# Column masks moved from VectorE to GpSimd, and a tile's shares from two VectorE operations to one on ScalarE

## The chip, the cores and the metric

One core of one Trainium2 chip runs the kernel. Engines are named as in the profile: PE (TensorE; PEld are its weight loads), DVE (VectorE), ACT (ScalarE), POOL (GpSimd) and SP (SyncE, which issues plain DMAs). Times are device microseconds of one execution; less is better. Before the change, nine runs have a median of 751.92 us (750.51 to 753.59).

## The reference

Two things are computed from the same normalized rows and added to the input: a selective scan over rows sorted by cluster, and a mixture of eight experts of which each token takes its two best.

```python
xn = _layernorm(x)                       # x: (2, 2048, 256)
# scan, d_state 16, per batch, in the order of the clusters
buckets = argmax(l2norm(xn) . l2norm(means)); sort_idx = argsort(buckets, stable)
u = xn[sort_idx].T
x_dbl = x_proj_weight @ u
dts, Bm, Cm = split(x_dbl, [32, 16, 16]);  Cm += (means @ prompt_weight.T)[buckets].T
delta = softplus(dt_projs_weight @ dts + bias);  A = -exp(A_logs)
h = exp(delta * A) * h + (delta * u) * Bm        # for each step, 256 channels x 16 states
y = sum over states of h * Cm,  + Ds * u,  back in the order of the tokens
# experts, 8, hidden 512
logits = xn @ w_gate;  top2, sel = top_k(logits, 2);  probs = softmax(top2)
e_out = (silu(xn @ w1) * (xn @ w3)) @ w2         # for the chosen experts
out = x + y + sum of probs * e_out
```

All values are float32.

## The kernel before

**The front (about the first 100 us).** Rows are normalized and written to a DRAM tensor `xn_d` of 256 + 4 columns. Each token's cluster and its two experts are found. `route` gives the pairs of token and expert places in 71 tiles of 128 rows (`NT`), each tile of one expert; inside it `find_weights` (L579) finds each tile's expert, and with it `te8` (the expert's index minus 8), and `find_shares` (L600) finds the two softmax weights of each token. `find_shares` puts four numbers in the last four columns of a row: first expert (minus 8), second weight, first weight minus second weight, second expert. 68 tiles (`n_dealt`) are always run; the last three stand in a conditional branch.

**A tile of the experts (`Tile`, L909).** Its weights come by two indirect DMAs of POOL (`load_up`, `load_down`, L914), its rows by another (`load_rows`, L928). `turn` (L933) transposes the rows on PE, ACT copies them (`xT`, L939), and two DVE operations find `own`, the weight of each row: `(first expert == this tile's) * (first - second) + second` (L941, L945). `up` does 16 matmuls for each half (L954), with a tanh on ACT (L962) and two DVE operations (`silu` L967, `gate` L971); `down` does 8 (L977), ACT scales the result with `own` into `yo` (L981), and POOL adds it to the output by an indirect DMA (L895). There are three weight buffers: `load_up` of tile t+3 follows `up` of tile t. There are four row buffers, three of `yo`, six of `own`.

**The scan (`Piece`, L638, and `Step`, L824).** A piece is 512 positions of one batch; there are eight. A piece has eight steps: four groups `q` of four states, for each half `h` of the channels. A step's four states each need `da` on ACT (L834), a product `bu` (L840) and a scan (L849) on DVE. The results of a step lie interleaved in `hs`; PE turns them (L861), ACT copies them (`ht`, L865), and PE contracts them with C (L870). For that contraction C stands in `z`, a tile of 128 x 512 for each `q`: partition p holds the C of state p mod 4 for all positions (`load_z`, L686, a broadcast DMA of SP), and `mask_z` (L695, the multiplication is L697) makes it zero outside the columns of that partition's own position within a group of 32. There is one buffer for each `q`, so the load for the next piece waits for the last contraction with the old one.

**The order.** `keep_order` (L126) makes every engine, POOL and SP among them, follow the order of the text. The main loop goes over 256 places (64 steps of four). At each place it emits a product, a scan, a part of the step before, then what `plan` has for that place, then as many parts of tiles (`jobs`: the first half of `up`, the second half, `down`) as a planner allows: `at_place` sums an estimate of PE and DVE time for each place (`on_pe`, `on_dve`; a mask counts 0.6 of DVE), and a part is dealt while PE's sum is under `ratio` times DVE's. Masks of the next piece stand at places 22, 27, 33 and 41 of a piece (L1135), those of the first at places 5, 6, 14 and 22 of the whole loop (L1146 to L1149). The `gather` of the next piece's rows (L632) is four more indirect DMAs of POOL, and `add_sums` another four.

Of the kernel before, what the change touches and what calls it, by code (L numbers as in the profile page):

```python
# [48 lines left out]
P = 128  # L49
# [7 lines left out]
def scan_moe_kernel(  # L57
# [27 lines left out]
    TS = P  # L85
    NT = (2 * B * L - E) // TS + E
    SH = 4
    HC = CH // 2
    BJ = B * J
    assert K == E == 8 and R == 32 and L % CH == 0 and H == CH  # L90
# [450 lines left out]
    def route():  # L541


        oh = oh_e
        (m1, m2), (i1, i2) = best, which
        (m1, m2), (i1, i2) = best, which
        cum = sml.tile([P, E, BJ], F32, tag="cum2", name="cum2")
        nc.vector.tensor_tensor_scan(
            cum.rearrange("p e j -> p (e j)"), keep2.rearrange("p e j -> p (e j)"),
            both.rearrange("p e j -> p (e j)"), 0.0, ALU.mult, ALU.add,  # L550
        )
        tot = sml.tile([P, E], F32, tag="tot2", name="tot2")
        nc.vector.tensor_copy(tot, cum[:, :, BJ - 1])
        pn = ps_m.tile([P, 2 * E], F32, tag="m", name="pn2")
        nc.tensor.matmul(pn[:, 0:E], lhsT=before, rhs=tot, start=True, stop=True)
        nc.tensor.matmul(pn[:, E:], lhsT=ones, rhs=tot, start=True, stop=True)
        normalize(n_x - 1, False)
        n_i = sml.tile([P, E], I32, tag="n_i", name="n_i")
        nc.vector.tensor_scalar(n_i, pn[:, E:], float(TS - 1), None, ALU.add)
        nc.vector.tensor_scalar(  # L560
            n_i, n_i, TS.bit_length() - 1, None, ALU.logical_shift_right
        )
        nt = sml.tile([P, E], F32, tag="nt", name="nt")
        nc.vector.tensor_copy(nt, n_i)
        end = sml.tile([P, E], F32, tag="end", name="end")
        nc.vector.tensor_tensor_scan(end, ones[:, 0:E], nt, 0.0, ALU.mult, ALU.add)
        base = sml.tile([P, E], F32, tag="base2", name="base2")
        nc.vector.tensor_sub(base, end, nt)
        nc.vector.tensor_scalar(base, base, float(TS), -1.0, ALU.mult, ALU.add)
        nc.vector.tensor_add(base, base, pn[:, 0:E])  # L570
        nc.vector.tensor_tensor(cum, cum, over(base, BJ), ALU.add)
        at = sml.tile([P, 2, BJ, E], F32, tag="at", name="at_slot")
        for i in range(2):
            nc.vector.tensor_mul(at[:, i], oh[:, i], cum.rearrange("p e j -> p j e"))
        sf = sml.tile([P, 2, BJ], F32, tag="sf", name="sf")
        nc.vector.tensor_reduce(sf, at, AX.X, ALU.add)
        slot = sml.tile([P, 2 * BJ], I32, tag="slot", name="slot")
        nc.vector.tensor_copy(slot, sf.rearrange("p i j -> p (i j)"))
        def find_weights():  # L579

            ge = sml.tile([P, NT, E], F32, tag="ge", name="ge")
            nc.vector.tensor_tensor(
                ge, over(idx_t, E), end.unsqueeze(1).to_broadcast([P, NT, E]), ALU.is_ge
            )
            te = sml.tile([P, NT], F32, tag="te", name="te")
            nc.vector.tensor_reduce(te, ge, AX.X, ALU.add)
            nc.vector.tensor_scalar_min(te, te, float(E - 1))
            nc.vector.tensor_scalar(te8, te, -float(E), None, ALU.add)
            nc.vector.tensor_copy(n_used, end[:, E - 1 : E])

            held = sml.tile([P, NT], F32, tag="held", name="held")
            nc.vector.memset(held[:, 0:NW], 0.0)
            nc.vector.tensor_tensor(held[:, NW:], te[:, NW:], te[:, : NT - NW], ALU.is_equal)
            nc.vector.tensor_scalar(held, held, float(E * P), row_p, ALU.mult, ALU.add)
            nc.vector.scalar_tensor_tensor(w_row, te, float(P), held, ALU.mult, ALU.add)  # L595
            for t in tiles[: NW - 1]:
                t.load_up()
                t.load_down()

        def find_shares():  # L600

            share = sml.tile([P, BJ, SH], F32, tag="share", name="share")
            nc.vector.tensor_copy(share[:, :, 0], i1)
            nc.vector.tensor_copy(share[:, :, 3], i2)
            nc.vector.tensor_sub(m2, m2, m1)
            nc.vector.tensor_mul(m2, m2, rstd)
            nc.scalar.activation(m2, m2, AF.Exp)
            nc.vector.tensor_scalar_add(m1, m2, 1.0)
            nc.vector.reciprocal(m1, m1)
            nc.vector.tensor_mul(share[:, :, 1], m2, m1)  # L610
            nc.vector.tensor_sub(share[:, :, 2], m1, share[:, :, 1])
            for b in range(B):
                nc.sync.dma_start(
                    xn_d[b * L : (b + 1) * L, D:].rearrange("(p j) c -> p j c", j=J),
                    share[:, b * J : (b + 1) * J, :],
                )

        tokens = list_tokens(
            slot, [m * LC // J % B for m in range(2 * BJ // LC)], NT, "e", front_factors,
            [lambda: None, find_shares, lambda: None, find_weights] + [lambda: None] * 3  # L620
            + [lambda: counts.extend(count_members())],
        )
        none = sml.tile([P, NT], F32, tag="none", name="none")
        nc.vector.tensor_scalar(none, tokens, 0.0, spare, ALU.is_equal, ALU.mult)
        nc.vector.scalar_tensor_tensor(token_of, tokens, -1.0, none, ALU.add, ALU.add)
# [12 lines left out]
    class Piece:  # L638
# [55 lines left out]

        def mask_z(self, q: int):  # L695
            z = self.zs[q]
            nc.vector.tensor_mul(z, z, mask.unsqueeze(1).to_broadcast([P, CH // G, G]))  # L697

        def load_b(self, q: int, parts: int = 1):
            bt = scn.tile([P, Q, CH], F32, tag="b", name="bt")  # L700
# [208 lines left out]
    class Tile:  # L909
# [23 lines left out]
        def turn(self):  # L933
            xg = self.xg
            pt = ps_m.tile([P, ND, P], F32, tag="m", name="pt_g")
            for h in range(ND):
                nc.tensor.transpose(pt[:, h, :], xg[:, h * P : (h + 1) * P], ident)
            self.xT = ffn.tile([P, ND, TS], F32, tag="xT", name="xT")
            nc.scalar.copy(self.xT, pt)  # L939
            self.own = ffn.tile([P, 1], F32, tag="own", name="own", bufs=6)  # L940
            nc.vector.scalar_tensor_tensor(  # L941
                self.own, xg[:, D : D + 1], te8[:, self.t : self.t + 1], xg[:, D + 2 : D + 3],
                ALU.is_equal, ALU.mult,
            )
            nc.vector.tensor_add(self.own, self.own, xg[:, D + 1 : D + 2])  # L945

        def up(self, i: int):
            wk = w13_sb[self.t % NW][:, i * ND * H : (i + 1) * ND * H].rearrange(
# [168 lines left out]
    for n, p in enumerate(pieces):  # L1117
        s0 = n * SP_
        for q in range(1, NQ):
            at_place(max(s0 + 2 * q - 3, 0), NSUB - 1 if n or q > 1 else 0, lambda p=p, q=q: p.load_b(q))  # L1120
        if n:
            s1 = s0 - SP_
            at_place(max(s1 - 1, 0), 1 if n > 1 else 0, p.gather)

            at_place(s1 + 3, 2, lambda p=p: behind_down.append(p.size), 1.1)
            for h in range(ND):
                at_place(s1 + 1, 2 + h, lambda p=p, h=h: p.turn(h), 0.5)
                at_place(s1 + 2, 1 + 2 * h, lambda p=p, h=h: p.project(h), 0.55)
                at_place(s1, 18 + 2 * h, lambda p=p, h=h: p.decay_of_one(h))
            at_place(s1, 23, p.log)  # L1130
            for i, place in enumerate((23, 24, 26, 28)):
                at_place(s1, place, lambda p=p, i=i: p.series(i), 0.0, 1.1)
            at_place(s1 + 2, 0, p.find_members, 0.0, 0.5)
            at_place(s1 + 3, 0, p.end_projection, 0.55)
            for q, load, use in ((0, 16, 22), (1, 20, 27), (2, 29, 33), (3, 37, 41)):  # L1135
                at_place(s1, load, lambda p=p, q=q: p.load_z(q))
                at_place(s1, use, lambda p=p, q=q: p.mask_z(q), 0.0, 0.6)
            at_place(s1 + 5, NSUB - 1, lambda p=p: p.load_b(0))
            at_place(s0, 3, lambda p=p: p.begin(0), 0.9)
            at_place(s0 + 1, 1, lambda p=p: p.begin(1), 0.9)  # L1140
        s2 = s0 + SP_
        at_place(s2, 0, lambda p=p: p.take_sums(0))
        if n + 1 < len(pieces):
            at_place(s2, 3, lambda p=p: p.take_sums(1))
            at_place(s2 + 1, 0, p.add_sums)
    at_place(1, 1, lambda: pieces[0].mask_z(0), 0.0, 0.6)  # L1146
    at_place(2, 3, lambda: list_rows(1, pos), 2.5, 4.0)
    for q in range(1, NQ):
        at_place(2 * q - 1, 2, lambda q=q: pieces[0].mask_z(q), 0.0, 0.6)  # L1149

    for n in range(NSUB * len(steps)):
        on_dve[n] += 1.75
# [129 lines left out]
```

## Time and profile before

| | us |
|---|---|
| median of nine runs | 751.92 |
| the profiled execution | 752.49 |
| its span, first to last instruction | 750.7 |
| mean granted TensorE clock | 0.953 |

| group (whole span) | count | busy us | mean ns |
|---|---|---|---|
| DVE scans L849 | 256 | 323.9 | 1281 and 1219 |
| DVE products L840 | 256 | 173.1 | 677 |
| PE matmuls of `up` L954 | 2176 | 272.6 | 281 |
| ACT `da` L834 | 256 | 183.6 | 734 |
| ACT `ht` L865 | 256 | 138.3 | 595 |
| POOL adds to the output L895 | 100 | 197.5 | 1927 and 2077 |
| POOL weight loads L914 | 136 | 185.9 | 1353 and 1382 |
| POOL row loads of tiles L928 | 68 | 91.4 | 1344 |

How to read the profile: "busy" is the time in which an engine has an instruction under way; matmuls and DVE operations overlap their neighbours a little, so what an operation costs is the time from its start to the next one's. A POOL indirect DMA is busy while POOL prepares it; the bytes arrive later. In a timeline a line is: start, length, engine, source line, operation, output and inputs with their shapes, count, and in brackets how long the engine was idle before and what ended that ("issue" is nothing that the profile shows).

### The profile page before, as it was taken

How to read it: one execution, taken by the hardware profiler on the slowest of the kernel's cores; microseconds unless marked ns; L12 is line 12 of the kernel's file. 1: busy time of each engine (PE TensorE's matmuls, PEld its weight loads, DVE VectorE, ACT ScalarE, POOL GpSimd, SP SyncE). 2: the span in 40 equal slices, each digit the busy share in tenths (PEclk: the TensorE clock that was granted, in tenths of full speed). 3: DMA queues.
4: the chain of work that ended last, by engine and by line, in shares of the span. 5: the costliest groups of instructions: out<-in, count | busy, mean ns of one | idle time of the engine just before them, and what ended most of it. 6: DMA issues, size and time to landing. Idle time of an engine off the chain costs nothing. (4 is left out here: it accounts for less than half of the span.)

```text
span 750.7 us, 16877 instructions
## 1 busy us (share of the span) xinstructions
PE 677.5 (90%) x6506; PEld 588.9 (78%) x6506; DVE 678.9 (90%) x1085; ACT 508.6 (68%) x983; POOL 522.2 (70%) x362
## 2 busy tenths in 40 slices
PE   7465779999998999999999999999999998999993
PEld 5234678788877898788878898998798977899982
DVE  8876399899987999999999999999999996999992
ACT  4831446686758866886769577967795767767762
POOL 2023548667777788777877887788788888677734
PEclk9755979999999999999999999999999999999998
DMA  8576554584435745685468546864585547735312
GB/s 269 227 162 244 162 171 92 159 257 133 126 55 163 254 144 121 171 270 140 113 141 271 164 128 122 269 189 127 122 251 155 136 84 224 233 109 120 87 17 29
DMA packets 60401, 120.31 MB, mean 160 GB/s; under 512 B 24160, under 2 KB 41248, under 8 KB 53152
## 3 DMA queue, kind: packets, MB, share of 16 engines
q0 software_dynamic: 38784, 63.71, 35.5%
q1 hardware_dynamic: 21536, 55.50, 21.9%
q8 instruction: 52, 0.85, 0.5%
q14 instruction: 29, 0.24, 0.1%
HBM read 170.78 MB, written 22.28 MB: 257 GB/s over the span
## 5 line engine op out<-in xcount | busy, mean ns | idle before, releaser
L954 PE MATMUL p_ps<-xT,w 128*128 128x128 f32 x2176 | 272.6, 281 | 12.3 <-DVE g L971 8.1
L954 PEld LDWEIGHTS p_ps<-xT,w 128*128 128x128 f32 x2176 | 258.0, 195 | 26.3 <-DVE g L971 8.3
L849 DVE TENSOR_TENSOR_SCAN hs<-da,carry,bu 128x512 f32<-128x512 f32 x192 | 245.9, 1281 | 0.0
L834 ACT ACTIVATE da<-dl,na 128x512 f32<-128x512 f32 x256 | 183.6, 734 | 0.2 <-DVE dl L789 0.2
L840 DVE TENSOR_TENSOR bu<-du,bt 128x512 f32<-128x512 f32 x256 | 173.1, 677 | 0.0
L865 ACT COPY ht<-pt_s 128x512 f32<-128x512 f32 x256 | 138.3, 595 | 39.1 <-PE pt_s L861 38.1
L895 POOL DMA_INDIRECT out_dram<-yo,token_of x68 | 131.0, 1927 | 46.8 <-ACT yo L981 20.2
L914 POOL DMA_INDIRECT w<-in_w_up_dram,w_row x68 | 92.0, 1353 | 93.7 <-DVE w_row L595 44.6
L861 PE MATMUL pt_s<-ident,hs 128*128 128x128 f32 x1024 | 135.9, 276 | 9.4 <-ACT ht L865 8.6
L977 PE MATMUL py<-w,g 128*128 128x256 f32 x544 | 129.8, 381 | 8.0 <-ACT xT L939 4.8
L861 PEld LDWEIGHTS pt_s<-ident,hs 128*128 128x128 f32 x1024 | 116.0, 141 | 20.9 <-ACT ht L865 13.4
L977 PEld LDWEIGHTS py<-w,g 128*128 128x128 f32 x544 | 98.0, 190 | 21.1 <-ACT xT L939 6.0
L928 POOL DMA_INDIRECT xg_sb<-xn,token_of x68 | 91.4, 1344 | 26.2 <-issue 12.2
L914 POOL DMA_INDIRECT w<-in_w_down_dram,w_row x68 | 93.9, 1382 | 20.7 <-issue 15.2
L895 POOL DMA_INDIRECT out_dram<-yt,line_of x32 | 66.5, 2077 | 20.8 <-issue 10.9
L849 DVE TENSOR_TENSOR_SCAN hs<-da,bu 128x512 f32<-128x512 f32 x64 | 78.0, 1219 | 0.0
L962 ACT ACTIVATE t_sb<-p_ps 128x512 f32<-128x512 f32 x68 | 41.0, 603 | 53.7 <-PE p_ps L954 53.5
L870 PE MATMUL y<-ht,z 128*32 128x128 f32 x2048 | 73.8, 277 | 1.8 <-PEq L1208 0.7
L981 ACT ACTIVATE yo<-py,own 128x256 f32<-128x256 f32 x68 | 32.3, 475 | 62.1 <-PE py L977 60.8
L967 DVE SCALAR_TENSOR_TENSOR t_sb<-t_sb,p_ps 128x512 f32<-128x512 f32 x68 | 45.8, 674 | 26.4 <-ACT t_sb L962 26.4
L870 PEld LDWEIGHTS y<-ht,z 128*32 128x32 f32 x2048 | 50.8, 109 | 19.8 <-issue 10.4
L632 POOL DMA_INDIRECT xs<-xn,line_of x32 | 41.8, 1306 | 14.7 <-issue 8.8
(202 smaller groups left out, 583.3 us busy)
## 6 DMA issues: line engine op xcount, KB each, us to landing
bt<-bc SPq DMA_DIRECT2D x31, 1024.0 KB, 5.1
z<-bc SPq DMA_DIRECT2D x32, 256.0 KB, 4.8
xn<-xt SPq DMA_DIRECT2D x8, 520.0 KB, 2.6
xt<-in_x_dram SPq DMA_DIRECT2D x8, 512.0 KB, 7.5
out_dram<-in_x_dram SPq DMA_DIRECT2D x8, 512.0 KB, 8.3
w<-in_w_up_dram,w_row POOLq DMA_INDIRECT x68, 3.9
w<-in_w_down_dram,w_row POOLq DMA_INDIRECT x68, 7.7
xg_sb<-xn,token_of POOLq DMA_INDIRECT x68, 4.5
```

The source lines that it names most:

```text
L834: nc.scalar.activation(self.da[i], self.piece.dl[:, self.h, :], AF.Exp, scale=na[:, self.h, n : n + 1])
L840: nc.vector.tensor_mul(self.bu[i], self.piece.du[:, self.h, :], self.piece.bts[self.q][:, i, :])
L849: nc.vector.tensor_tensor_scan(self.hs[:, :, i], self.da[i], self.bu[i], start, ALU.mult, ALU.add)
L861: nc.tensor.transpose(pt[:, j, :], self.hs[:, t0 : t0 + G, :].rearrange("p t n -> p (t n)"), ident)
L865: nc.scalar.copy(self.ht[i], pt)
L870: nc.tensor.matmul(p.ys[self.h][j * G : (j + 1) * G, i, :], lhsT=p.zs[q][:, i * (P // G) + j, :], rhs=self.ht[i][:, j, :], start=False, st ...
L895: ins = nc.gpsimd.indirect_dma_start(out=out_rows, out_offset=bass.IndirectOffsetOnAxis(ap=numbers, axis=0), in_=rows, in_offset=None, com ...
L914: nc.gpsimd.indirect_dma_start(out=to[self.t % NW], out_offset=None, in_=rows, in_offset=bass.IndirectOffsetOnAxis(ap=w_row[:, self.t : se ...
L928: nc.gpsimd.indirect_dma_start(out=self.xg, out_offset=None, in_=xn_d, in_offset=bass.IndirectOffsetOnAxis(ap=token_of[:, self.t : self.t ...
L954: nc.tensor.matmul(p[:, f, :], lhsT=wk[:, h, f * P : (f + 1) * P], rhs=self.xT[:, h, :], start=h == 0, stop=h == ND - 1,)
L967: nc.vector.scalar_tensor_tensor(self.s, self.s, 1.0, self.p1, ALU.add, ALU.mult)
L977: nc.tensor.matmul(py, lhsT=self.g[:, f, :], rhs=w2[:, f, :], start=f == 0, stop=f == NH - 1)
```

## The change

Three things change. `mask_z` is issued on GpSimd instead of VectorE, at the same places of the written order, and the planner is no longer told of 0.6 of DVE time for it. `own` becomes one ScalarE operation, `Identity(scale * first expert's column + bias)` with the tile's `te8` as scale: a straight line in the expert's index that passes through the first weight at the first expert and the second weight at the second. For that, `find_shares` writes the slope and the offset of that line into the first two of the four columns, which takes eleven VectorE operations instead of eight, and `te8` is the index minus 3.5 (`MID` is 4.5).

```diff
+    MID = (E + 1) / 2
...
-            nc.vector.tensor_scalar(te8, te, -float(E), None, ALU.add)
+            nc.vector.tensor_scalar(te8, te, MID - E, None, ALU.add)
...
             share = sml.tile([P, BJ, SH], F32, tag="share", name="share")
-            nc.vector.tensor_copy(share[:, :, 0], i1)
-            nc.vector.tensor_copy(share[:, :, 3], i2)
             nc.vector.tensor_sub(m2, m2, m1)
             nc.vector.tensor_mul(m2, m2, rstd)
             nc.scalar.activation(m2, m2, AF.Exp)
+            nc.vector.tensor_sub(share[:, :, 3], i1, i2)
+            nc.vector.reciprocal(share[:, :, 3], share[:, :, 3])
             nc.vector.tensor_scalar_add(m1, m2, 1.0)
             nc.vector.reciprocal(m1, m1)
-            nc.vector.tensor_mul(share[:, :, 1], m2, m1)
-            nc.vector.tensor_sub(share[:, :, 2], m1, share[:, :, 1])
+            nc.vector.tensor_mul(share[:, :, 2], m2, m1)
+            nc.vector.tensor_sub(m1, m1, share[:, :, 2])
+            nc.vector.tensor_mul(share[:, :, 0], m1, share[:, :, 3])
+            nc.vector.scalar_tensor_tensor(m1, i2, MID, share[:, :, 0], ALU.add, ALU.mult)
+            nc.vector.tensor_sub(share[:, :, 1], share[:, :, 2], m1)
...
         def mask_z(self, q: int):
             z = self.zs[q]
-            nc.vector.tensor_mul(z, z, mask.unsqueeze(1).to_broadcast([P, CH // G, G]))
+            nc.gpsimd.tensor_tensor(z, z, mask.unsqueeze(1).to_broadcast([P, CH // G, G]), ALU.mult)
...
-            nc.vector.scalar_tensor_tensor(
-                self.own, xg[:, D : D + 1], te8[:, self.t : self.t + 1], xg[:, D + 2 : D + 3],
-                ALU.is_equal, ALU.mult,
-            )
-            nc.vector.tensor_add(self.own, self.own, xg[:, D + 1 : D + 2])
+            nc.scalar.activation(
+                self.own, xg[:, D : D + 1], AF.Identity, bias=xg[:, D + 1 : D + 2],
+                scale=te8[:, self.t : self.t + 1],
+            )
...
-                at_place(s1, use, lambda p=p, q=q: p.mask_z(q), 0.0, 0.6)
+                at_place(s1, use, lambda p=p, q=q: p.mask_z(q))
...
-    at_place(1, 1, lambda: pieces[0].mask_z(0), 0.0, 0.6)
+    at_place(1, 1, lambda: pieces[0].mask_z(0))
...
-        at_place(2 * q - 1, 2, lambda q=q: pieces[0].mask_z(q), 0.0, 0.6)
+        at_place(2 * q - 1, 2, lambda q=q: pieces[0].mask_z(q))
```

## The prediction

> **What bounds the kernel now.** I read the page's shares first.
>
> ```profile
> PE 677.5 (90%) x6506; PEld 588.9 (78%) x6506; DVE 678.9 (90%) x1085; ACT 508.6 (68%) x983; POOL 522.2 (70%) x362
> ```
>
> These are averages over a front without the scan and a long loop, so the loop comes next, in three stretches (busy us of PE, PEld, DVE, ACT, POOL, each with its count).
>
> ```profile
> 100.00:350.00 250.00, 237.85 (x2314) 211.46 (x2313) 233.27 (x337) 175.49 (x346) 188.92 (x124) 0.99 0.56 157
> 350.00:625.00 275.00, 268.52 (x2737) 236.72 (x2736) 268.93 (x374) 204.79 (x399) 224.80 (x142) 1.00 0.62 165
> 625.00:725.00 100.00, 96.51 (x969) 87.56 (x968) 94.51 (x131) 70.85 (x133) 71.42 (x46) 0.98 0.52 132
> ```
>
> From 350 to 625 us PE and DVE are both 98% busy, and ACT 74%. POOL looks free at 82%, but its timeline shows 0.30 us before nearly every DMA: 224.8 + 142 x 0.30 = 267.4 of 275 us. POOL has 7.6 us left in that stretch; three engines are full there, not two. In the first stretch it has 250 - 188.9 - 124 x 0.30 = 24 us.
>
> Why POOL's DMAs are so long is seen by laying its timeline beside DVE's. First POOL:
>
> ```profile
> 113.07 1.91 POOL L914 DMA_INDIRECT w<-in_w_down_dram,w_row  x1 [0.30 <-issue]
> 115.29 0.98 POOL L914 DMA_INDIRECT w<-in_w_up_dram,w_row  x1 [0.31 <-issue]
> ...
> 122.11 1.17 POOL L914 DMA_INDIRECT w<-in_w_up_dram,w_row  x1 [0.31 <-issue]
> 123.58 3.66 POOL L928 DMA_INDIRECT xg_sb<-xn,token_of  x1 [0.30 <-issue]
> ```
>
> and DVE at those moments:
>
> ```profile
> 112.91 1.22 DVE L849 TENSOR_TENSOR_SCAN hs<-da,bu 128x512 f32<-128x512 f32 x1
> ...
> 114.96 0.68 DVE L967 SCALAR_TENSOR_TENSOR t_sb<-t_sb,p_ps 128x512 f32<-128x512 f32 x1
> ...
> 123.53 1.21 DVE L849 TENSOR_TENSOR_SCAN hs<-da,bu 128x512 f32<-128x512 f32 x1
> 124.67 0.65 DVE L840 TENSOR_TENSOR bu<-du,bt 128x512 f32<-128x512 f32 x1
> 125.25 1.21 DVE L849 TENSOR_TENSOR_SCAN hs<-da,bu 128x512 f32<-128x512 f32 x1
> ```
>
> The weight load at 113.07 begins in a scan that ends at 114.13 and lasts until 0.85 us after it; the one at 115.29 begins beside L967, whose second input is in PSUM, and takes 0.98 us. The row load at 123.58 loses three rounds. Over the loop, 246 POOL DMAs that begin under a DVE operation with both inputs in SBUF are 0.51 us longer than the shortest of their kind; 40 that begin beside L967 or L971 are never over 0.05 us longer. So **DVE's two-SBUF-input work and POOL's SBUF reads exclude each other**. Over all 316 DMAs that is 0.40 us each.
>
> **The change, part by part.** The sum starts from the profiled execution, 752.49 us (span 750.7 and 1.8 around it; 0.6 over the median of the runs).
>
> *Masks off DVE.* 32 multiplications of 128x512, mean 664 ns, but each starts 0.58 us before the next DVE operation (294.45 to 295.03): 32 x 0.58 = 18.6 us off DVE.
>
> *Shares off DVE.* L941 and L945 take 0.31 us together from start to start (295.03 to 295.34). 65 of 68 pairs lie in the loop: 20.2 us off DVE.
>
> ```profile
> L697 DVE TENSOR_TENSOR z<-z,mask 128x512 f32<-128x512 f32 x32 | 21.2, 664 | 0.0
> L941 DVE SCALAR_TENSOR_TENSOR own<-xg_sb,te 128x1 f32<-128x1 f32 x68 | 13.8, 203 | 0.0
> L945 DVE TENSOR_TENSOR own<-own,xg_sb 128x1 f32<-128x1 f32 x68 | 10.8, 159 | 2.3
> masks.py:199 POOL TENSOR_SCALAR_AFFINE_SELECT ident<-ident 128x128 f32<-128x128 f32 x1 | 0.3, 293 | 0.1
> ```
>
> *Masks on POOL: their own length.* No such multiplication is in the trace. Low end: DVE's 0.66 us. The nearest POOL row that reads and writes f32 is the select above, 0.293 us for 128 columns, so four times that, 1.17 us, for 512. High end: 1.17 us and the lost rounds above (3.66 - 0.95 = 2.71 us), 3.9 us. I take 1.15 us, next to the select.
>
> *What they take from DVE.* A mask reads two SBUF tensors for all of its length, so I let it hold DVE off that long, in the share of cases where DVE's next operation has two SBUF inputs (246 of 316, some 0.8): 32 x 1.15 x 0.8 = 29 us back on DVE; bounds 0 (no exclusion in this direction) and 37 us. DVE's net is -18.6 - 20.2 + 29 = -10 us. PE, 96% busy over these 625 us, limits what this is worth; I credit 4 us (bounds 0 and, without exclusion, PE's idle of 22).
>
> The Trainium skill's page "GPSIMD Engine Reference", "Performance versus the Vector engine", gives about 2.6 cycles an element to a two-input operation on GpSimd and advises against it; by it a mask would be about 1.17 us, an estimate. Its page "SBUF — State Buffer", "Who interferes with whom", says that a DVE instruction with two SBUF inputs and a GpSimd instruction that reads SBUF block each other for the whole instruction; the trace shows one direction of this, and by the page DVE would lose some 37 us to the masks, which leaves next to nothing of the relief.
>
> *What they take from POOL.* Each adds 0.30 (gap) + 0.40 (mean wait for DVE) + 1.15 = 1.85 us. They stand in the written order, mostly behind a tile's weight load; behind each wait the row gathers, the adds and the next weight loads. 14 masks fall in 350 to 625: 25.9 us, less 2.5 us of DMA waits that DVE's masks caused (0.52 us at 11 starts in all, 14 of 32 masks). Against 7.6 us free, POOL falls 16 us behind there, and some 4 us before. What is late next is the up weights: in 440 to 600 us they are issued 12.7 to 14 us ahead of their first use by PE, and land in 3.9 us (median), so about 9 us can be absorbed. 20 - 9 = 11 us would reach PE; a stalled PE lets DVE idle and shortens POOL's waits, so I take 7.5 us. Bounds: at 0.66 us a mask (c = 1.36) POOL falls 9 us behind in the stretch and nothing reaches PE; the high end is worked out as a rival.
>
> *The first mask.* POOL's order puts it behind the up load that ends at 123.28. PE first uses that z at 121.32 (the first contraction, PE's timeline):
>
> ```profile
> 121.32 1.08 PE L870 MATMUL y<-ht,z 128*32 128x128 f32 x32
> ```
>
> 123.3 + 0.4 + 1.15 = 124.8: PE waits 3.5 us, behind it the next tile and the next turns. DVE idles 2.3 + 1.0 us at 133 to 135 anyway, so I count 2.5 us (0 to 6, if it loses rounds as the DMA at 123.58 did). The second is reached at 131 and used at 144; from the second piece on masks come 40 us or more before their use. Their z is loaded over 10 us earlier (issued at 283.17, masked at 294.45 on DVE, reached by POOL after 305): no wait on SP's queue.
>
> *Shares on ACT.* One ACTIVATE of one column with pointer scale and bias: L429 has that form at 256 columns, 587 ns, one every 0.495 us; L855, four columns without pointers, 195 ns. I take 0.28 us: 65 x 0.28 = 18 us on ACT, 72% busy in the loop. But all 20 us of waits that PE's queue shows in the loop end on ACT, and copies of ht stand behind the new instruction. Bounds 0 and 6 us (a third of the 18); I take 2. What hides the rest is ACT's idle time, its waits for PE.
>
> *Front.* The shares get five new DVE operations (0.22, 0.39 for a reciprocal, 3 x 0.25) and lose two copies (0.17); 0.30 of it fits in the wait for Exp: +0.9, taken as 0.8, since DVE is dense behind it (0 to 1). The pairs there (71.68 to 72.32) precede 4 us of waiting: nothing.
>
> *The planner.* Without 0.6 for each mask its DVE total goes from 597.0 to 577.8; following its sums, 122 of 197 tile parts move, mostly by one place, at most four. All still fit: 0, within 2 either way.
>
> Sum: 752.5 - 4 + 7.5 + 2.5 + 2 + 0.8 = **761 us**, slower by 1.2%. Its own range, with POOL's term from 0 to 20: 753 to 774.
>
> **Rivals.**
>
> 1. *POOL's lateness never reaches PE; relief wins.* For: today PE waits for no weights. Against: 7.6 us free. With 7 of DVE's 10 us credited, and 1 each for the first mask and ACT: 752.5 - 7 + 1 + 1 + 0.8 = 748 us. It decides if c stays under 1.4 us.
> 2. *DVE is not held by a mask.* Then DVE loses 39 us of work, PE's 22 us of idle can shrink by 15, and the first mask and ACT cost 3: 752.5 - 15 + 3 + 0.8 = 741 us. Against: the exclusion of the timelines.
> 3. *A mask is starved as the DMA at 123.58 was.* 2.5 us each, c = 3.2: 14 x 3.2 - 10 = 35 us in the middle stretch and, with some 21 us usable before it, 14 x 3.2 - 2.5 - 21 = 21 before; 56 - 9 = 47, of which PE's stalls return a third: 752.5 + 31 = 783 us. Against: only 11 of the 246 starts lost a further round.
> 4. *The share on ACT is not one operation but brings table loads*, 1.283 us each (L743, L834). For: Ln and Exp alternate there. Against: Identity (L739) runs between Exps without one. At most 7 more: 761 + 4 = 765 us.
>
> **How the numbers follow.** Forecast 0.50 (slower 0.47, same 0.03); rival 1 0.18 (faster 0.14, same 0.04); rival 2 0.08, faster; rival 3 0.16, slower; rival 4 0.08 (slower 0.07, same 0.01). About 0.2% can be told from no change here. Faster 0.22, same 0.08, slower 0.70. The range 743 to 784 leaves out most of rival 2 and the upper half of rival 3, some 0.15.
>
> **What would show it.** Masks on POOL of about 1.15 us plus waits; DVE scans or products near 2.3 us at 32 places; POOL without free time from 350 to 625 and PE waiting for w there; PE waiting for z at 121 us; one ACT instruction of 0.2 to 0.4 us for each tile and no more table loads. It is wrong if DVE's operations keep their length beside a mask, or if PE never waits for a weight.

## The result, and the profile after

| | before | after |
|---|---|---|
| median, us | 752.13 (62 runs) | 805.37 (20 runs, 799.87 to 812.25) |
| ratio, 95% | | 1.0702 (1.0682 to 1.0721) |
| profiled execution, us | 752.49 | 812.37 |
| its span, us, and granted clock | 750.7, 0.953 | 810.6, 0.924 |

The change costs 53 us, against a forecast of 8.5 and a range that ended at 784. Ratios, here and below, come from undisturbed runs alone, and so differ a little from the quotients of the medians beside them; the profiled executions of after and of after_again are not among these and lie 7 us above their medians. First the engines' shares of after, then three stretches of its loop (busy us of PE, PEld, DVE, ACT, POOL, each with its count, then clock, DMA share and GB/s).

```profile
PE 696.2 (86%) x6506; PEld 601.5 (74%) x6506; DVE 673.7 (83%) x920; ACT 527.6 (65%) x1051; POOL 586.7 (72%) x394
```

```profile
100.00:350.00 250.00, 223.23 (x2076) 196.21 (x2076) 207.87 (x246) 164.59 (x338) 191.44 (x121) 0.93 0.47 133
350.00:625.00 275.00, 250.52 (x2453) 221.73 (x2451) 239.83 (x270) 196.43 (x388) 227.44 (x139) 0.96 0.57 157
625.00:725.00 100.00, 91.48 (x895) 79.57 (x897) 88.30 (x101) 68.85 (x141) 81.27 (x53) 0.97 0.60 166
```

From 350 to 625 us DVE has fallen from 98% to 87% and PE from 98% to 91%; POOL is as busy as before. DVE was relieved of 165 instructions and is hardly less busy for it: 673.7 us in all, after 678.9. Both now wait. The waits of PE in the loop (us in total, times, longest), in which before had none for a DMA or for `z`:

```profile
PE p_ps L958 <- DMA w<-in_w_up_dram,w_row: 16.9, 4, 10.6
PE pt_u L658 <- DMA xs<-xn,line_of: 12.1, 8, 3.2
...
PE y L875 <- POOL z L702: 8.6, 1, 8.6
...
PE py L981 <- DMA w<-in_w_down_dram,w_row: 3.6, 4, 1.6
```

All four are POOL's deliveries: 41 us. By the start of each step's first scan, after lies 11 us behind before at the 4th step of 64 (behind the first mask), 12 at the 12th, 19 at the 20th, 34 at the 36th and 57 from the 52nd on: the loss builds up over most of the loop.

The groups (busy us, mean ns, then idle before):

```profile
L854 DVE TENSOR_TENSOR_SCAN hs<-da,carry,bu 128x512 f32<-128x512 f32 x192 | 254.0, 1324 | 0.0
L845 DVE TENSOR_TENSOR bu<-du,bt 128x512 f32<-128x512 f32 x256 | 192.7, 753 | 0.0
...
L854 DVE TENSOR_TENSOR_SCAN hs<-da,bu 128x512 f32<-128x512 f32 x64 | 78.1, 1221 | 0.0
...
L702 POOL TENSOR_TENSOR z<-z,mask 128x512 f32<-128x512 f32 x32 | 42.3, 1323 | 0.8
L946 ACT ACTIVATE own<-xg_sb,te 128x1 f32<-128x1 f32 x68 | 27.0, 397 | 0.0
```

A mask takes 1.32 us on POOL, a share 0.40 us on ACT. Scans and products sum to 524.8 us, 27.8 more than before. Where that comes from is seen at one mask; POOL first, then DVE at that time (start, length):

```profile
333.58 1.03 POOL L919 DMA_INDIRECT w<-in_w_down_dram,w_row  x1 [0.30 <-issue]
334.63 1.28 POOL L702 TENSOR_TENSOR z<-z,mask 128x512 f32<-128x512 f32 x1
336.08 1.30 POOL L919 DMA_INDIRECT w<-in_w_up_dram,w_row  x1 [0.16 <-issue]
```

```profile
333.56 0.66 DVE L975 SCALAR_TENSOR_TENSOR g<-t_sb,p_ps 128x512 f32<-128x512 f32 x1
334.14 2.33 DVE L845 TENSOR_TENSOR bu<-du,bt 128x512 f32<-128x512 f32 x1
336.40 1.27 DVE L854 TENSOR_TENSOR_SCAN hs<-da,carry,bu 128x512 f32<-128x512 f32 x1
```

The weight load got in beside L975, whose second input is in PSUM, and the mask followed it after 0.02 us. The product at 334.14 is held until the mask ends at 335.91, and lasts 2.33 us instead of 0.67.

The first mask, on POOL, DVE and PE:

```profile
121.72 3.91 POOL L919 DMA_INDIRECT w<-in_w_down_dram,w_row  x1 [0.30 <-issue]
125.93 1.00 POOL L919 DMA_INDIRECT w<-in_w_up_dram,w_row  x1 [0.31 <-issue]
126.96 1.27 POOL L702 TENSOR_TENSOR z<-z,mask 128x512 f32<-128x512 f32 x1
```

```profile
121.85 1.21 DVE L854 TENSOR_TENSOR_SCAN hs<-da,bu 128x512 f32<-128x512 f32 x1
122.98 0.65 DVE L845 TENSOR_TENSOR bu<-du,bt 128x512 f32<-128x512 f32 x1
123.57 1.21 DVE L854 TENSOR_TENSOR_SCAN hs<-da,bu 128x512 f32<-128x512 f32 x1
```

```profile
128.28 1.94 PE L875 MATMUL y<-ht,z 128*32 128x128 f32 x32 [8.59 <-POOL z L702]
```

The mask itself is not late by its own length: the weight load two places ahead of it met three DVE operations in a row with both inputs in SBUF, and lasts 3.91 us instead of 1.0.

The longest single wait of PE, 10.6 us, has the same root. POOL, then part of DVE, then PE:

```profile
581.33 7.95 POOL L900 DMA_INDIRECT out_dram<-yt,line_of  x1 [0.31 <-ACT ht L870]
589.58 2.05 POOL L900 DMA_INDIRECT out_dram<-yt,line_of  x1 [0.30 <-issue]
591.93 5.61 POOL L900 DMA_INDIRECT out_dram<-yt,line_of  x1 [0.30 <-issue]
597.85 1.55 POOL L900 DMA_INDIRECT out_dram<-yt,line_of  x1 [0.30 <-issue]
599.70 1.07 POOL L919 DMA_INDIRECT w<-in_w_up_dram,w_row  x1 [0.30 <-issue]
```

```profile
581.28 1.27 DVE L854 TENSOR_TENSOR_SCAN hs<-da,carry,bu 128x512 f32<-128x512 f32 x1
...
586.61 1.27 DVE L854 TENSOR_TENSOR_SCAN hs<-da,carry,bu 128x512 f32<-128x512 f32 x1
587.81 0.65 DVE L971 SCALAR_TENSOR_TENSOR t_sb<-t_sb,p_ps 128x512 f32<-128x512 f32 x1
```

```profile
602.37 6.54 PE L958 MATMUL p_ps<-xT,w 128*128 128x128 f32 x32 [10.62 <-DMA w<-in_w_up_dram,w_row]
```

The add that begins at 581.33 waits through seven scans and products without a gap and gets in beside L971, the first operation with an input in PSUM. It takes 7.95 us where the shortest add takes 1.55. The up weights stand behind it. In before, the loop had 6 POOL DMAs that were over 1.4 us longer than the shortest of their kind (14 us in all); in after 15 (44 us). I count as a lost round a boundary between two DVE operations at which a POOL DMA was waiting and the next DVE operation, with two inputs in SBUF, went first: 16 before, 37 after (good to a few, since it depends on where in its time a DMA is taken to have got in). So the masks explain the 28 us of held DVE time; they don't by themselves explain why the DMAs lose more often.

### The profile page after: what moved, and what is told of

Same layout as the page of the kernel before. It is cut to its first block, busy times and chain, and to the rows that moved or that the text cites. A ratio compares the mean times of both kernels' runs of the same rounds, so it can differ in the third digit from the quotient of the medians.

```text
span 810.6 us, 16862 instructions
## 1 busy us (share of the span) xinstructions
PE 696.2 (86%) x6506; PEld 601.5 (74%) x6506; DVE 673.7 (83%) x920; ACT 527.6 (65%) x1051; POOL 586.7 (72%) x394
## 5 line engine op out<-in xcount | busy, mean ns | idle before, releaser
L958 PE MATMUL p_ps<-xT,w 128*128 128x128 f32 x2176 | 279.0, 286 | 31.0 <-DMA w<-in_w_up_dram,w_row 16.9
L958 PEld LDWEIGHTS p_ps<-xT,w 128*128 128x128 f32 x2176 | 265.4, 200 | 44.5 <-issue 24.8
L854 DVE TENSOR_TENSOR_SCAN hs<-da,carry,bu 128x512 f32<-128x512 f32 x192 | 254.0, 1324 | 0.0
L845 DVE TENSOR_TENSOR bu<-du,bt 128x512 f32<-128x512 f32 x256 | 192.7, 753 | 0.0
L919 POOL DMA_INDIRECT w<-in_w_up_dram,w_row x68 | 94.3, 1387 | 87.5 <-DVE w_row L596 45.3
L919 POOL DMA_INDIRECT w<-in_w_down_dram,w_row x68 | 104.2, 1532 | 20.7 <-issue 17.1
L971 DVE SCALAR_TENSOR_TENSOR t_sb<-t_sb,p_ps 128x512 f32<-128x512 f32 x68 | 45.8, 673 | 83.6 <-ACT t_sb L966 83.5
L933 POOL DMA_INDIRECT xg_sb<-xn,token_of x68 | 86.8, 1277 | 24.4 <-issue 17.0
L900 POOL DMA_INDIRECT out_dram<-yt,line_of x32 | 80.1, 2503 | 15.9 <-issue 8.2
L875 PE MATMUL y<-ht,z 128*32 128x128 f32 x2048 | 76.7, 285 | 10.1 <-POOL z L702 8.6
L875 PEld LDWEIGHTS y<-ht,z 128*32 128x32 f32 x2048 | 52.9, 112 | 29.1 <-issue 11.1
L975 DVE SCALAR_TENSOR_TENSOR g<-t_sb,p_ps 128x512 f32<-128x512 f32 x68 | 45.5, 670 | 7.5 <-PE p_ps L958 6.0
```

What stands on the lines that cost most here:

```text
L845: nc.vector.tensor_mul(self.bu[i], self.piece.du[:, self.h, :], self.piece.bts[self.q][:, i, :])
L854: nc.vector.tensor_tensor_scan(self.hs[:, :, i], self.da[i], self.bu[i], start, ALU.mult, ALU.add)
L875: nc.tensor.matmul(p.ys[self.h][j * G : (j + 1) * G, i, :], lhsT=p.zs[q][:, i * (P // G) + j, :], rhs=self.ht[i][:, j, :], start=False, st ...
L900: ins = nc.gpsimd.indirect_dma_start(out=out_rows, out_offset=bass.IndirectOffsetOnAxis(ap=numbers, axis=0), in_=rows, in_offset=None, com ...
L919: nc.gpsimd.indirect_dma_start(out=to[self.t % NW], out_offset=None, in_=rows, in_offset=bass.IndirectOffsetOnAxis(ap=w_row[:, self.t : se ...
L933: nc.gpsimd.indirect_dma_start(out=self.xg, out_offset=None, in_=xn_d, in_offset=bass.IndirectOffsetOnAxis(ap=token_of[:, self.t : self.t ...
```

## The experiments

The kernel before takes between 752 and 767 us on different chips, so each kernel is compared with before on its own chip, by ratio. The expectations of e1 to e4 give times as on a chip where before takes 752 us; theirs takes 766.59. Where operations were added, nothing reads their outputs. The diffs are excerpts, with comments added.

**1. Either part alone, and the planner.** Masks alone; shares alone; after with only the very first mask back on DVE; after with the planner told 0.6 for a mask, as before.

```diff
 e1_masks_only: before with
+            nc.gpsimd.tensor_tensor(z, z, mask.unsqueeze(1).to_broadcast([P, CH // G, G]), ALU.mult)
 (and at_place without 0.6)
 e2_shares_only: after with the masks on nc.vector and at_place with 0.0, 0.6
 e3_first_on_dve: after with
+            if self is pieces[0] and q == 0:
+                nc.vector.tensor_mul(z, z, mask.unsqueeze(1).to_broadcast([P, CH // G, G]))
 e4_plan_kept: after with
+                at_place(s1, use, lambda p=p, q=q: p.mask_z(q), 0.0, 0.6)
```

> Before, with only the masks moved to POOL (planner told as in the change); the shares stay two DVE operations. Theory A (the masks fill POOL's queue and its lateness reaches PE) and theory B (each mask holds DVE off): the masks carry nearly all of the 53 us, 795 to 805 us, and DVE products and scans longer by 29 us in sum as in the changed kernel. Rival C (the small DVE operations of the shares were the openings at which POOL's DMAs got at SBUF, and without them POOL starves): clearly less, 770 to 785 us, with no POOL DMA over 4 us beyond its shortest.

> The changed kernel with the masks back on DVE and in the planner's sums; only the shares move to ACT. If DVE sets the loop's pace: 20 us less of DVE work, faster, 738 to 748 us. Rival C (POOL starves without the small DVE operations): slower, 756 to 775 us, with POOL DMAs of several us more than before. Rival D (ACT's later copies hold PE): 754 to 758 us, PE's waits for ht and xT longer than the 20 us of before, POOL's DMAs unchanged.

> The changed kernel with the very first mask alone back on DVE. The trace shows PE waiting 8.6 us for it and DVE 10 us behind. If that wait is paid in full: 795 to 797 us. If it only comes before other waits that then take its place (POOL behind anyway): 801 to 804 us.

> The changed kernel with the planner still told of 0.6 of DVE time for each mask, so that the parts of tiles stand at the places of before. If the new places matter (rival F): under 798 us. If not: 801 to 808 us.

| | us | before there | ratio (95%) |
|---|---|---|---|
| e1_masks_only | 788.74 | 766.59 | 1.0250 (1.0184 to 1.0316) |
| e2_shares_only | 779.97 | 766.59 | 1.0148 (1.0083 to 1.0213) |
| e3_first_on_dve | 786.45 | 766.59 | 1.0268 (1.0196 to 1.0339) |
| e4_plan_kept | 798.17 | 766.59 | 1.0418 (1.0339 to 1.0496) |

Both parts cost, and the shares, which take work off a full DVE, cost 1.5% without any mask on POOL. Taking the first mask off POOL gave some 12 us against e4 (798.17 to 786.45), which differs from e3 by the planner too; the two intervals just touch, and without the shares (e9 against e1, below) it is 0.8%, 6 us. The waits of PE in the loop of e2_shares_only:

```profile
PE pt_u L658 <- DMA xs<-xn,line_of: 5.3, 3, 2.9
...
PE p_ps L958 <- DMA w<-in_w_up_dram,w_row: 3.5, 3, 2.3
```

Here too PE waits for POOL's deliveries, with no more work on POOL than before. It has 25 lost rounds, and its DMAs that are over 1.4 us too long sum to 27 us; e1_masks_only has 12 and 12 us. So the shares alone lengthen the DMAs, and the masks alone don't. But long DMAs are not the whole cost: e4, with both parts, has only 7 of them (16 us), about as before, and its ratio is 1.0418 all the same; PE waits there 25 us for POOL's deliveries and 4 us for the first `z`.

**2. What a mask does: POOL's time or its reads.** Before, with something else on POOL at the 32 places: a memset that reads nothing, or a multiplication of two constant tiles.

```diff
 e5_pool_memset:
+            nc.gpsimd.memset(idle, 0.0)          # idle: 128 x 1400
 e6_pool_multiply:
+            nc.gpsimd.tensor_tensor(other, some, mask.unsqueeze(1).to_broadcast([P, CH // G, G]), ALU.mult)
```

> Before, with one memset on POOL (128 x 1400, about 1.3 us by the memsets of the front, written and never read) at each of the 32 mask places; masks and shares stay on DVE. It takes POOL's time as a mask does, but reads nothing from SBUF. Theory A (POOL's time in its full queue): ratio over 1.015. Theory B (the masks' reads hold DVE off): ratio under 1.005, DVE's products as long as before (677 ns).

> Before, with a multiplication on POOL of the same form as a mask (two constant SBUF tiles, 128 x 512, into a tile that nothing reads) at each of the 32 mask places; masks and shares stay on DVE. Theory A: the same ratio as with the memset. Theory B: over that by DVE's held time, 29 us, so a ratio of 1.03 to 1.06, with DVE products and scans longer by some 29 us in sum. Nothing waits for its result, so the first mask's wait is absent.

> The changed kernel unaltered, for its ratio on the chip of these runs, where the kernel before may take another time than 752 us. All theories: ratio 1.05 to 1.07.

| | us | before there | ratio (95%) | scans and products, us |
|---|---|---|---|---|
| e5_pool_memset | 774.37 | 765.55 | 1.0149 (1.0088 to 1.0210) | 496.9 |
| e6_pool_multiply | 784.37 | 765.55 | 1.0288 (1.0201 to 1.0374) | 519.2 |
| after_again (after, unaltered) | 799.25 | 765.55 | 1.0442 (1.0341 to 1.0543) | 521.2 |

The groups of e5 and of e6 (as above):

```profile
L698 POOL MEMSET idle<- 128x1400 f32 x32 | 41.1, 1283 | 0.1
```

```profile
L698 POOL TENSOR_TENSOR other<-some,mask 128x512 f32<-128x512 f32 x32 | 46.1, 1439 | 0.9
```

The memset is nearly as long as a mask, and DVE's operations keep their sum to 0.1 us (before 497.0): a POOL operation that only writes doesn't hold DVE. It costs 1.5% by POOL's time alone. The multiplication holds DVE for 22 us. The two costs can't simply be subtracted: in e5 PE waits 8.2 us for late DMAs, in e6 1.2 us. The ratio of after_again, 1.0442, lies below what was expected, though its interval reaches into that range.

**3. Why the shares cost: ACT's time, or DVE's two small operations.** The share on ACT with the old pair still run into an unread tile; the share as one DVE operation; the share on ACT and one memset on DVE.

```diff
 e7_shares_both: e2_shares_only with
+            nc.vector.scalar_tensor_tensor(unused, xg[:, D : D + 1], te8[:, self.t : self.t + 1], xg[:, D + 2 : D + 3], ALU.is_equal, ALU.mult)
+            nc.vector.tensor_add(unused, unused, xg[:, D + 1 : D + 2])
 e8_share_one_dve: e2_shares_only with
+            nc.vector.tensor_scalar(self.own, xg[:, D : D + 1], te8[:, self.t : self.t + 1], xg[:, D + 1 : D + 2], ALU.mult, ALU.add)
 e10_shares_and_memset: e2_shares_only with
+            nc.vector.memset(unused, 0.0)        # one column
```

> The kernel with the shares on ACT and the masks on DVE, plus the two small DVE operations of before into a tile that nothing reads. Rival C (the small operations are openings for POOL): back to the ratio of before, within 0.5%, and POOL DMAs with no long starvation. Rival D (the share's place on ACT costs): ratio 1.015 or more, as without them.

> The share as a straight line in the expert's index, but as one DVE operation in place of two; masks on DVE and in the planner's sums as before. It keeps a small DVE operation for each tile, and frees some 0.15 us of DVE for each. If small operations are POOL's openings and DVE's time counts: ratio 0.992 to 0.998, faster than both kernels, no POOL DMA starved more often than before. If one small operation opens less than two: 1.000 to 1.008.

> The shares on ACT and the masks on DVE (ratio 1.015 in its own run), plus one memset of one column on DVE for each tile, which reads nothing. If any operation that doesn't read two SBUF tensors opens SBUF for POOL: 1.000 to 1.006. If it takes the longer pair of the two old operations: 1.010 or more.

| | us | before there | ratio (95%) | lost rounds |
|---|---|---|---|---|
| e7_shares_both | 768.01 | 765.55 | 1.0040 (1.0001 to 1.0078) | 15 |
| e8_share_one_dve | 771.24 | 764.93 | 1.0090 (1.0052 to 1.0127) | 35 |
| e10_shares_and_memset | 772.66 | 764.93 | 1.0119 (1.0077 to 1.0161) | 29 |

With the pair back, ACT's operation and the longer front together cost 0.4%, and PE waits for no DMA. So ACT is not it; what is missed is the pair. One small operation in its place, whether it reads the row (e8) or nothing (e10), doesn't replace it, and PE waits for row gathers and weights in both (6.4 and 4.4 us). For e8 that lies above both expectations. Lost rounds don't measure the time: e8 has 35 where e2 has 25, and costs no more than e2.

The pair in the trace of before. POOL, then DVE:

```profile
371.88 3.71 POOL L895 DMA_INDIRECT out_dram<-yt,line_of  x1 [0.30 <-issue]
```

```profile
372.32 1.27 DVE L849 TENSOR_TENSOR_SCAN hs<-da,carry,bu 128x512 f32<-128x512 f32 x1
373.51 0.65 DVE L697 TENSOR_TENSOR z<-z,mask 128x512 f32<-128x512 f32 x1
374.10 0.20 DVE L941 SCALAR_TENSOR_TENSOR own<-xg_sb,te 128x1 f32<-128x1 f32 x1
374.33 0.16 DVE L945 TENSOR_TENSOR own<-own,xg_sb 128x1 f32<-128x1 f32 x1
374.41 0.69 DVE L840 TENSOR_TENSOR bu<-du,bt 128x512 f32<-128x512 f32 x1
```

Every operation here starts before its predecessor's end (373.51 under the scan that ends at 373.59), except L945: it needs L941's result, and between 374.30 and 374.33 DVE is empty. The add on POOL ends at 375.59, 1.26 us after that. Of 42 POOL DMAs that had been under way for at least 0.5 us when an L945 began, 35 end at a fixed distance from it, weight and row loads after 0.63 to 0.75 us and adds after 1.25 to 1.31.

That distance doesn't show that they went in during the pause. Measured from the end of the scan before, weight loads that had been waiting end after 0.80 to 0.85 us where L941 follows the scan, 0.79 to 0.84 where L967 or L971 follows, and 0.79 to 0.87 where another operation with two SBUF inputs follows; adds after 1.39 to 1.41, 1.35 to 1.42 and 1.35 to 1.41. In e12 below, without a pause, weight loads end 0.77 to 0.87 us behind such a scan too. So these DMAs went in at the end of the operation ahead of L941, before the pause, as others do elsewhere. One such place in before, with two SBUF inputs on either side, POOL and then DVE:

```profile
120.36 1.45 POOL L914 DMA_INDIRECT w<-in_w_down_dram,w_row  x1 [0.30 <-issue]
```

```profile
120.24 0.66 DVE L840 TENSOR_TENSOR bu<-du,bt 128x512 f32<-128x512 f32 x1
120.82 1.23 DVE L849 TENSOR_TENSOR_SCAN hs<-da,bu 128x512 f32<-128x512 f32 x1
```

The load ends 0.91 us after the product does; it didn't have to wait for the scan. What sets the pair apart is how surely a DMA gets in. In a count of its own, beside the lost rounds, I take the DMAs that wait at the end of a DVE operation with two SBUF inputs, and say that those got in that end 0.80 to 1.06 us (adds 0.6 us later) after the start of the operation that follows. Where L941 follows, all 35 get in in before; where L967 or L971 follows, all 34; where another operation with two SBUF inputs follows, 136 of 150. In after, without the pair, the last figure is 135 of 175.

**4. The dependent pair by itself.** The share on ACT and two one-column operations on DVE: the second reads the first, or neither reads anything. Then the dependent pair added to after.

```diff
 e11_dependent_pair: e2_shares_only with (e14_after_dependent_pair: after with)
+            nc.vector.memset(unused, 0.0)
+            nc.vector.tensor_scalar_add(unused, unused, 1.0)
 e12_two_memsets: e2_shares_only with
+            nc.vector.memset(unused[:, 0:1], 0.0)
+            nc.vector.memset(unused[:, 1:2], 0.0)
```

> The shares on ACT and the masks on DVE, plus on DVE for each tile a memset of one column and an addition to the same column, which waits for the memset. If the pause between two dependent operations is POOL's opening: ratio 1.000 to 1.006 and few lost rounds (12 to 16, as before). If it takes two operations that read two SBUF tensors: 1.010 or more, 25 lost rounds or more.

> The same with two memsets of one column each that don't depend on each other. If the pause is the opening: 1.010 or more, as with one memset, and 25 lost rounds or more. If two small operations in a row are enough: 1.000 to 1.006.

> The changed kernel plus, on DVE for each tile, a memset of one column and a dependent addition to it. If the missing pause costs beside the masks what it costs alone (0.0148 of ratio with the shares on ACT against 0.9998 with the pause): from 1.044 to 1.025 to 1.031. If POOL's fullness by the masks hides it: 1.038 or more.

| | us | before there | ratio (95%) | lost rounds |
|---|---|---|---|---|
| e11_dependent_pair | 764.39 | 765.36 | 0.9998 (0.9964 to 1.0031) | 11 |
| e12_two_memsets | 772.26 | 765.36 | 1.0120 (1.0082 to 1.0158) | 18 |
| e14_after_dependent_pair | 780.45 | 751.90 | 1.0364 (1.0306 to 1.0421) | 12 |

DVE of e11, then of e12:

```profile
382.92 0.06 DVE L951 MEMSET unused<- 128x1 f32 x1
383.01 0.15 DVE L952 TENSOR_SCALAR unused<-unused 128x1 f32<-128x1 f32 x1
383.08 0.68 DVE L845 TENSOR_TENSOR bu<-du,bt 128x512 f32<-128x512 f32 x1
```

```profile
314.64 0.69 DVE L845 TENSOR_TENSOR bu<-du,bt 128x512 f32<-128x512 f32 x1
314.66 0.06 DVE L951 MEMSET unused<- 128x1 f32 x1
314.67 0.06 DVE L952 MEMSET unused<- 128x1 f32 x1
```

In e11 DVE is empty from 382.98 to 383.01; in e12 the memsets run under the product. With the dependent pair the whole 1.5% of the shares is gone and PE waits for no DMA; with two independent operations 1.2% stays. The pair does no useful work. In the trace of e11 all 29 DMAs that wait where the pair follows get in, and 133 of 141 where another operation with two SBUF inputs follows. How the dependence brings this about the traces don't show. e12 can't be read for it: its profiled execution, 765.52 us, is the fastest of its runs (the others 770.82 to 776.33), so its 18 lost rounds, where 25 or more were expected, are not those of a usual run. Nor is the pair the only thing that sets how many lose: e4, without it, has 136 of 152 getting in where another such operation follows, as before has.

In after the pair gives 1.036, on a chip where before takes 751.9 us. Where after alone gave 1.070, before took 752.1 us, which would make the pair worth 3.4%, about 25 us; but after was not run on the chip of e14, and from the 1.0442 of after_again it is only 0.8%, with intervals that overlap. The result lies between the two expectations; PE still waits 8.5 us for the first `z` there.

**5. The first mask without the shares, and a pause elsewhere.** Masks alone with the very first on DVE; and e8 with the copy of a step's last column (`carry`) moved from ACT to DVE, right behind the scan it reads.

```diff
 e9_masks_not_first: e1_masks_only with
+            if self is pieces[0] and q == 0:
+                nc.vector.tensor_mul(z, z, mask.unsqueeze(1).to_broadcast([P, CH // G, G]))
 e13_carry_on_dve: e8_share_one_dve with
+                nc.vector.tensor_copy(carry[:, self.q, self.h, :], self.hs[:, CH - 1, :])
```

> Masks alone on POOL (ratio 1.025 in its own run), with the very first mask back on DVE; the shares stay on DVE. If the first mask's wait (10.4 us at PE's queue) is paid in full: 1.010 to 1.014. If POOL's lateness takes its place: 1.020 or more.

> The share as one DVE operation (ratio 1.009 in its own run), and the copy of a step's last column moved from ACT to DVE, right behind the scan that it depends on, 48 times. If any dependent operation opens SBUF for POOL: 0.995 to 1.003, lost rounds 10 to 18. If not, or if DVE's time sets the pace: 1.009 or more.

e9 gave 777.80 against 764.93 us, 1.0170 (1.0103 to 1.0237), between the two expectations (one run of 2839 us is left out); PE waits there 11.1 us for up weights, so part of what the first mask cost is only taken over. e13 gave 768.40 against 751.90 us, 1.0215 (1.0178 to 1.0253), with 33 lost rounds: a miss. Its group shows a pause like the pair's, 1.7 us over 48:

```profile
L860 DVE COPY carry<-hs 128x4 f32<-128x4 f32 x48 | 8.6, 178 | 1.7
```

So a pause is not enough. In the trace of e13, of its fastest run, all 12 DMAs that wait where the copy follows get in, but where another operation with two SBUF inputs follows only 103 of 134 do, fewer than in before; that a DMA gets in at the place put in doesn't settle how the rest fare. The copy follows a long scan, stands at other places (ends of steps) and occurs 48 times and not 68; which of these decides was not tried. And e8 ran on a chip where before takes 764.93 us, so that 1.0215 against its 1.0090 is no clean comparison.

## Why the prediction was wrong

The direction was right (slower, 0.70), and so was the mechanism of the masks: POOL has no time left and shuts out DVE as DVE shuts out POOL. The time was wrong by 44 us. The forecast's own steps, in its order:

- ***Masks off DVE* and *what they take from DVE*: right.** 29 us of held DVE time were forecast, 27.8 measured (27.0 in e1, none in e5). The Trainium skill's "SBUF — State Buffer", "Who interferes with whom", says that a two-input DVE instruction contends with a GpSimd instruction that reads SBUF and not with one that only writes it; e5 and e6 agree, 0.1 us of held time against 22.
- ***Shares off DVE*: the step that failed.** "20.2 us off DVE" was booked as relief, with nothing on the other side but ACT's 2 us and the front. By the forecast's own terms (4 us credited for 10 off DVE) the shares alone should have gained some 5 us, an estimate: 8 credited, less 2 and 0.8. They cost 1.5%, 11 us, in e2: with no more work on POOL its DMAs come late and PE waits for them. A dependent pair of no use wins it back (e11, 0.9998), two independent operations don't (e12, 1.0120). So the two small operations were worth more to POOL than their 20 us to DVE; how their dependence does this stays open. The forecast looked for what lets a waiting DMA go at L967 and L971 only; at L941 too each of 35 got in. For the masks alone the same terms give some 14 us, an estimate (7.5 + 2.5 + 4 for 29 - 18.6 = 10 us on DVE), and e1 measured 2.5%, 19 us (14 to 24): the forecast broke at the shares and not there. The step makes some 16 of the 44 us by these estimates; about 20 lie between the 1.070 and the 1.044 of two chips, for which no run shows a cause.
- ***Masks on POOL: their own length*: close.** 1.15 us taken, 1.32 measured. By the 2.6 cycles an element of the Trainium skill's "GPSIMD Engine Reference", "Performance versus the Vector engine", and the 1.2 GHz of that page, 512 elements are an estimated 1.11 us, not the 1.17 that the forecast gave; the shortest masks measured, 1.27, are 14% longer.
- ***What they take from POOL*: right in kind, the size too small.** 7.5 us were taken (0 to 20). POOL's time alone, e5, costs 1.5%, 11 us; the high end came from masks that are slow themselves, not from DMAs that get longer. And only up weights were named as late: of PE's 41 us, 12.1 are row gathers of the scan and 3.6 down weights.
- ***The first mask*: mis-sized.** 2.5 us (0 to 6); PE waits 8.6, in e1 10.4. The forecast gave the mask 0.4 us of waiting and took the two loads ahead of it at their lengths in the trace of before; DVE's order around them had changed, and one of them lost three rounds.
- ***Shares on ACT* and *front*: right.** 2 + 0.8 us taken; e7, which has both, costs 0.4%, 2.5 us (0.0 to 0.8%), although a share takes 0.397 us and not 0.28.
- ***The planner*: right as far as it can be seen.** Taken as 0; e4 at 1.0418 and after_again at 1.0442 differ by less than either's interval.

Of the rivals, the first (lateness never reaches PE) and the second (DVE not held) fall by PE's waits and by the 2.33 us product. The fourth (table loads) falls: one ACT operation for each share and no more table loads than before. The third (783 us, masks starved) is nearest by its time, but not by its mechanism: masks mostly run 1.27 to 1.29 us, the longest 1.95; what starves are the DMAs on either side of them.

What stays open: what the dependent pair does for POOL; why after costs 1.070 on one chip and 1.044 on another whose before is 1.8% slower (1.5% and 2.5%, the two parts alone on chips like the second, nearly make up the 1.044 but not the 1.070); how much of the granted clock's fall (0.99 to 0.93 from 100 to 350 us) follows PE's waits and how much adds to them; and e13. How the masks' own 2.5% divides among POOL's time, held DVE time, the first mask and the relief is argued from e1, e5, e6 and e9, whose intervals are as wide as the differences. No kernel that was run is faster than before; the best, e11, is the same.

## What to carry to other kernels

Before work is taken off a full engine, ask what its neighbour does around that work: two small operations of 20 us in all cost more to take away than they freed, and only a run of that part by itself showed it. Before work is moved onto GpSimd, add the gap ahead of each of its DMAs (0.30 us here) to its busy time, and follow what stands behind the new instruction in its order, down to the engine that uses it. To learn what lets a waiting DMA go, a fixed distance from one candidate to the DMAs' ends is not enough: compare it with the distance at other places, and count how many get in at each.

## What had not been expected of the hardware

- Two one-column operations on DVE, the second of which reads the first, take the cost of the shares away (0.9998 in e11), and two that are independent don't (1.0120 in e12). Why is not known; the DMAs that were waiting go in ahead of the pause between the two.
- A POOL DMA that waits at the end of a DVE operation with two SBUF inputs got in there every time in before if an operation with an input in PSUM (34) or L941 (35) came next, and 136 times of 150 if another with two SBUF inputs did; in after 39 of 39 and 135 of 175. The lost rounds add up where they follow each other: 7.95 us for an add that needs 1.55.
- A POOL multiplication behind a DMA starts nearly at once, not after the 0.30 us of a DMA (0.02 us at 334.63). The DVE product that begins at 334.14, before the mask, did not get done ahead of it: it ends 0.56 us after the mask.
